# Graph attention with three layer norms: later due times, a third row tile, and one shared turn for the softmax denominators of both head halves

## Chip, cores and metric

The kernel runs on one core of one Trainium2 chip. The metric is the device time of one execution in microseconds (us). Three timed runs of the kernel before gave 3237.86, 3241.72 and 3245.61 us; the median, 3241.72 us, is the time to beat. A fourth, separate execution was recorded by the hardware profiler, and all durations below come from that one.

## What is computed

The input `x` has 8 images of 2048 rows with 256 channels, and `adj` is a 2048 x 2048 adjacency matrix shared by all images. There are 8 heads of 32 channels. Everything is float32.

```python
qkv = einsum('fnc,ck->fnk', x, w_qkv)            # q, k, v, each (f, n, 8, 32)
scores = einsum('fnhd,fmhd->fhnm', q, k) / sqrt(32)
scores = where(adj > 0, scores, -1e9)
attn = softmax(scores, axis=-1)                  # over the 2048 neighbours m
t = einsum('fhnm,fmhd->fnhd', attn, v).reshape(F, N, C)
x1 = layernorm(x + t) * ln1_g + ln1_b
h = relu(x1 @ w1 + b1)
x2 = layernorm(x1 + h @ w2 + b2) * ln2_g + ln2_b
out = layernorm(x + x2)
```

The scores are computed for all pairs, masked, and never written to memory outside the core.

## The kernel before

**Tiling.** The main loop (L599) runs over 1024 *blocks*. A block is one choice of image `f` (8), chunk of 512 query rows `qc` (4), half of the heads `g` (2, four heads each) and 128 neighbours `mb` (16). So 16 blocks make a *half*, 32 blocks make a *chunk* and 128 blocks make an *image*. In each block TensorE makes the scores of four heads (L230, neighbours on the partitions, queries along the free axis), VectorE adds the mask while it takes them out of PSUM (L233, two instructions), ScalarE takes the exponential in place (L237), and TensorE multiplies by the values (L249), adding up in one PSUM bank over the 16 blocks of a half. Scores are issued two blocks ahead (`LEAD`), the exponential one block ahead.

**Denominators.** The softmax denominator is a sum of the exponentials over all 2048 neighbours. Of the 16 score tiles of a half, seven are added into the first one by GpSimd (`POOLED`, L271), two chains of four are added by accumulating DMAs that GpSimd issues (`MOVED`, L268), and one stands alone. The function `denominator` (L297) multiplies the four tiles that remain with a matrix of ones on TensorE (L315, four steps of four matmuls), copies the sum out with ScalarE (`dT`, L317), turns it with four transposes (L321) and takes reciprocals on VectorE (L326), with two small bookkeeping instructions (L327, L328). It does so once for each half, so twice per chunk. A score tile comes from a pool of 12 (`pp`), and the tiles that `denominator` reads are free only after it has read them.

**The row tail.** After the second half of a chunk, `outcome` (L333) turns the attention output (two transposes groups, L352), multiplies it by the reciprocals on VectorE (L353) into a row tile `y` of 512 rows, and GpSimd adds `x` to it with an accumulating DMA (L339). Then `tail` (L357) makes the first norm, the feed-forward (`feed_forward`, L449: two transposes groups, then two groups each for `w1` and `w2`), the second norm, two GpSimd multiplies and adds (L363, L365), another accumulating DMA (L367), the third norm and the store (L370). A norm (L274) takes four statistics on VectorE (L278, L279), a short chain on GpSimd (L283 to L287), and four activations on ScalarE (L290). There are two row tiles (`yp`), so at most two tails are open at once (`ROOM`, L530).

**The order of the work beside the main loop.** All of this, and the projections and transposes that prepare the next image, is written as generators that are kept in the list `fill`, sorted by a due time (L488). In each block `advance` (L504) resumes them. A number that a generator yields is the number of blocks until it goes on. `BANK` means that it needs the one PSUM bank that is left for such work, and a group of matmuls keeps the bank until it is through (`MORE`). `advance` gives each block a credit of 2200, and a step of four 512-column matmuls costs 2048, a group of transposes 1400; so a block takes one step, unless some generator that waits for the bank is past its due time: then the whole group is issued in that block. All engines execute their own instructions in the order in which this loop wrote them.

**Masks.** The mask tiles of the next chunk are loaded by SyncE (`load_mask`, L150), one in every second block of the second half (L600), into a pool of nine tiles (`mkp`); a chunk uses eight.

The lines that the change and the prediction speak of: `denominator` L297 to L331, `outcome` L333, `norm` L274 with its wait L288, `feed_forward` with its wait L472, `tail` with its wait L368, `ROOM` L530, `load_mask` L600, and the constants `SUM` L262 and L341 to L344.

Of the kernel before, what the change touches and what calls it, by code (L numbers as in the profile page):

```python
# [19 lines left out]
P = 128  # L20
H = 8
# [40 lines left out]
def fast_path(ctx, tc, cst, x, adj, out, RS):  # L62
# [5 lines left out]
    dp = ctx.enter_context(tc.tile_pool(name="dp", bufs=1, space=bass.MemoryType.DRAM))  # L68
    mkp = ctx.enter_context(tc.tile_pool(name="mkp", bufs=MB // 2 + 1))
    ld = ctx.enter_context(tc.tile_pool(name="ld", bufs=LD))  # L70
# [13 lines left out]

    ident, identb, wqkv, w1s, w2s = cst["ident"], cst["identb"], cst["wqkv"], cst["w1s"], cst["w2s"]
    state = {"pair": 0, "side": None, "turn": 0, "turned": False, "holder": None, "tails": 0, "credit": 0}
# [47 lines left out]
    def mask_blocks(qc, mc, cv, to=None):  # L134
        for half in range(2):
            yield BANK
            ps = bank(BF16)
            for r in range(2):
                for j in range(TPC):
                    rr = 2 * half + r  # L140
                    nc.tensor.transpose(ps[:, r, j * P:(j + 1) * P], cv[:, j, rr * P:(rr + 1) * P], identb)
            k = 2 * mc + half
            m = to[half] if to else mask_piece(0, qc, k)
            if half:
                nc.vector.tensor_tensor(m, ps, cst["ones"][:, 0:1, None].to_broadcast([P, 2, CH]), ALU.min, saturate=False)
            else:
                nc.scalar.copy(m.bitcast(I8), ps)
            nc.sync.dma_start(MD[qc, k], words(m))
# [70 lines left out]

    PT, O, OT, RC = {}, {}, {}, {}  # L220

# [39 lines left out]
    ENDED = MB - 5  # L261
    SUM = 4  # L262

# [10 lines left out]
    def norm(t, per=1):  # L274
# [12 lines left out]
        nc.gpsimd.tensor_scalar(nb, nb, -1.0, 1.0, op0=ALU.mult, op1=ALU.mult)  # L287
        yield 2  # L288
        for j in range(TPC):
# [7 lines left out]
    def denominator(f, qc, g, ready):  # L297
        grp = (f, qc, g)
        blocks = [ALONE] + [chain[0] for chain in MOVED + (POOLED,)]
        late = {len(blocks) - 1: ready}  # L300
        if (f, qc, g) == items[-1][:3]:
            blocks = [POOLED[0], 11, 12, MOVED[1][0], 13, 14, MOVED[0][0], 15]
            late = {n: len(items) - k for n, k in ((2, 2), (3, 1), (4, 1), (5, 0), (6, 0), (7, 0))}
        yield BANK
        ps = bank()
        for n, block in enumerate(blocks):
            if n:
                yield MORE
            while state["now"] < late.get(n, 0):
                yield WAIT  # L310
            term = PT.pop((f, qc, g, block))
            state["credit"] -= 4 * CH
            for h in range(4):
                r = D * h
                nc.tensor.matmul(ps[r:r + D, :], cst["ones"], term[:, h, :], start=(n == 0), stop=(n == len(blocks) - 1))  # L315
# [6 lines left out]
        if g == 0:  # L322
            RC[f, qc] = op.tile([P, TPC, H], F32, name="rc")
        rc = RC[f, qc]
# [4 lines left out]
        if g == 1:  # L329
            begin = items.index((f, qc, g, LAST)) + SUM + 2  # L330
            start(begin, outcome(f, qc) if (f, qc) != (F - 1, NCK - 1) else finish(f, qc), begin)  # L331

    def outcome(f, qc):  # L333
        yield ROOM
        state["tails"] += 1
        xin = x[f, qc * CH:(qc + 1) * CH, :].rearrange("(p j) c -> p j c", p=P)
        y = yp.tile([P, TPC, C], F32, name="y")
        yield from divide(f, qc, y)
        nc.gpsimd.dma_start(y, xin, accum_op=ALU.add)  # L339
        begin = items.index((f, qc, 1, LAST)) + SUM + 2  # L340
        if (f, qc) == (F - 1, NCK - 2):  # L341
            start(begin + 5, tail(f, qc, y, xin, 2), begin + 8)
        else:
            start(begin + 10, tail(f, qc, y, xin), begin + 26)  # L344

    def divide(f, qc, y):
        rc = RC.pop((f, qc))
        for gg in range(2):
# [5 lines left out]
                                    ps.rearrange("p (j h d) -> p j h d", h=4, d=D),  # L354
                                    rc[:, :, 4 * gg:4 * gg + 4, None].to_broadcast([P, TPC, 4, D]), ALU.mult)

    def tail(f, qc, y, xin, per=1):  # L357
# [9 lines left out]
        nc.gpsimd.dma_start(z, xin, accum_op=ALU.add)  # L367
        yield 7  # L368
        yield from norm(z, per)
# [67 lines left out]
    def finish(f, qc):  # L437
        y = yp.tile([P, TPC, C], F32, name="y")
        xr, xb = state["rows"]
# [4 lines left out]
        while both:  # L444
            for e in list(both):
                if next(e, both) is both:
                    both.remove(e)

    def feed_forward(y):  # L449
# [21 lines left out]
        state["turned"] = False  # L471
        yield 1  # L472
        z = y
# [30 lines left out]
    def advance(t, finish=False):  # L504
# [15 lines left out]
        for e in list(fill):  # L520
            while e[2] is not None and e[0] <= t and e is not state["holder"]:
# [14 lines left out]
    items = [(f, qc, g, mb) for f in range(F) for qc in range(NCK) for g in range(2) for mb in range(MB)]  # L536
    LEAD = 2
    FRAME = 2 * NCK * MB
# [221 lines left out]
def kernel(  # L760
# [47 lines left out]
    make_identity(nc, cst["ident"])  # L808
    cst["identb"] = const.tile([P, P], BF16, name="identb")
    nc.vector.tensor_copy(cst["identb"], cst["ident"])  # L810
    cst["ones"] = const.tile([P, D], F32, name="ones")
    nc.gpsimd.memset(cst["ones"], 1.0)
    cst["mhalf"] = const.tile([P, TPC], F32, name="mhalf")
    nc.gpsimd.memset(cst["mhalf"], -0.5)
    RS = const.tile([P, 2, TPC, H // 2], F32, name="RS")
    nc.gpsimd.memset(RS[:, 0], 0.0)
# [5 lines left out]
    with tc.tile_pool(name="gd", bufs=1) as gd, \  # L822
# [6 lines left out]
        ps = gdp.tile([2, 1], F32, name="okp")  # L829
        nc.tensor.matmul(ps, ok, cst["ones"][:, 0:1], start=True, stop=True)  # L830
# [3 lines left out]
        nc.tensor.matmul(ps1, n_ok, cst["ones"][0:2, 0:1], start=True, stop=True)  # L834
        bad = gd.tile([1, 1], I32, name="bad")
# [35 lines left out]
```

## Time and profile before

| | us |
|---|---:|
| median of three runs | 3241.72 |
| the profiled execution's own time | 3246.02 |
| its span (first to last instruction) | 3244.1 |
| start to the first block's value product | 98.9 |
| 1023 spacings from that one to the last block's value product | 3097.6 |
| from there to the end | 47.6 |
| mean and median spacing of two blocks | 3.03 and 2.92 |

The spacing of blocks is read off the starts of the value products (L249) in the timeline; an image is 128 of them. Image 0 took 373.8 us, images 1 to 6 took 388.4 us on average, and image 7 took 393.5 us. The granted TensorE clock was 0.985 of full speed over the span and 1.00 in most chunks.

### The profile page before, as it was taken

The page shows a single profiled execution, that of the slowest core. Times are in us where ns is not written, and L with a number is a line of the kernel's source. Part 1 is how long each engine was busy: PE and PEld are TensorE (multiplying, and loading weights), DVE is VectorE, ACT ScalarE, POOL GpSimd, SP SyncE. Part 2 cuts the span into 40 slices and gives each one's busy share as a digit, 9 for nine tenths or more (in the row PEclk, how much of TensorE's full clock was granted, in tenths as well). Part 3 has the DMA queues.
Part 4 walks back from the last instruction along what each step waited for, and adds up shares of the span by engine and source line. Part 5 has one row for each costly group of instructions (what it writes and reads, how often), then busy time and mean ns, then how long its engine had stood idle before and what let it go on. Part 6 is the DMA issues. An engine that isn't in the chain of part 4 may idle for free.

```text
span 3244.1 us, 68406 instructions
## 1 busy us (share of the span) xinstructions
PE 3109.4 (96%) x28996; PEld 979.0 (30%) x28996; DVE 2735.7 (84%) x3203; ACT 2435.8 (75%) x1941; POOL 2592.2 (80%) x1358
## 2 busy tenths in 40 slices
PE   7899999999999999999999999999999999998985
PEld 4222333223332233322233323323233323332222
DVE  4888888888888888888988888888888888888975
ACT  3667778777777777778777778777778777777774
POOL 0568888888878888788887888888888788878884
PEclk8899999999999999999999999999999999999998
DMA  9688779778879788788787879878788878877763
GB/s 320 145 181 185 183 176 199 178 177 196 181 176 207 171 188 193 159 195 200 178 181 174 185 174 221 177 167 198 173 192 197 177 168 198 181 171 161 166 145 86
DMA packets 153240, 590.52 MB, mean 182 GB/s; under 512 B 15040, under 2 KB 67776, under 8 KB 103904
## 3 DMA queue, kind: packets, MB, share of 16 engines
q0 software_dynamic: 64416, 434.80, 66.9%
q1 hardware_dynamic: 87696, 149.98, 13.1%
q8 instruction: 229, 3.75, 0.4%
q10 hardware_dynamic: 816, 1.31, 0.1%
q14 instruction: 83, 0.68, 0.1%
HBM read 146.67 MB, written 37.75 MB: 57 GB/s over the span
## 4 chain that ended last, share of the span: by engine, by line
PE 75%; DVE 7%; POOL 5%; issue 4%; DMA 4%; ACT 2%; DVEq 0%; POOLq 0%; ACTq 0%
PE s L230 27%; PE x L249 24%; PE x L54 14%; PE x L315 6%; DVE p L233 6%; PE x L95 4%; DMA p<-p 3%; POOL p L271 2%; ACT p L237 1%; DMA mask<-md 1%; POOL y L365 1%; DVE st L278 1%; POOL y L363 0%; POOL y L461 0%; POOL y L459 0%
## 5 line engine op out<-in xcount | busy, mean ns | idle before, releaser
L233 DVE TENSOR_TENSOR p<-s,mask 128x1024 f32<-128x1024 f32 x2048 | 2409.3, 1218 | 372.7 <-PE s L230 209.9
L237 ACT ACTIVATE p<-p 128x2048 f32<-128x2048 f32 x1024 | 1956.1, 1910 | 521.4 <-DVE p L233 465.6
L271 POOL TENSOR_TENSOR p<-p 128x2048 f32<-128x2048 f32 x381 | 1825.5, 4793 | 223.7 <-ACT p L237 221.3
L230 PE MATMUL s<-qT,kT 32*128 32x512 f32 x8192 | 1173.8, 643 | 40.8 <-DVE p L233 35.9
L249 PE MATMUL x<-p,v 128*32 128x512 f32 x8192 | 1096.0, 607 | 16.7 <-ACT p L237 16.4
L268 POOL DMA_DIRECT2D p<-p x383 | 359.3, 956 | 306.9 <-ACT p L237 88.3
L230 PEld LDWEIGHTS s<-qT,kT 32*128 32x128 f32 x8192 | 321.1, 183 | 644.7 <-DVE p L233 587.2
L249 PEld LDWEIGHTS x<-p,v 128*32 128x32 f32 x8192 | 161.6, 108 | 797.8 <-issue 310.6
L315 PE MATMUL x<-p,ones 128*32 128x512 f32 x2080 | 268.2, 594 | 17.9 <-POOL p L271 11.1
L290 ACT ACTIVATE y<-y,nb,rs 128x256 f32<-128x256 f32 x372 | 218.7, 590 | 40.4 <-POOL nb L287 40.4
L54 PE MATMUL x<-in,wqkv 128*32 128x512 f32 x1888 | 243.5, 592 | 0.0
L278 DVE BATCH_NORM_STATS2 st<-y 128x6 f32<-128x256 f32 x372 | 154.9, 416 | 5.1 <-DMA y<-in_x_dram 5.1
L54 PE MATMUL x<-turned,w1s 128*32 128x512 f32 x992 | 123.5, 596 | 0.4 <-ACT in L166 0.4
L54 PE MATMUL x<-w2s,hT 128*32 128x256 f32 x2016 | 121.8, 382 | 2.1 <-DVE y L483 2.1
L54 PEld LDWEIGHTS x<-wqkv,in 128*32 128x32 f32 x3584 | 102.2, 110 | 63.4 <-issue 58.9
L315 PEld LDWEIGHTS x<-p,ones 128*32 128x32 f32 x2080 | 66.3, 110 | 178.2 <-issue 140.4
L54 PE MATMUL x<-wqkv,in 128*32 128x128 f32 x3584 | 117.3, 273 | 0.0
L54 PEld LDWEIGHTS x<-in,wqkv 128*32 128x32 f32 x1888 | 61.7, 110 | 140.9 <-issue 113.7
L284 POOL TENSOR_TENSOR rs<-rs,mhalf 128x4 f32<-128x4 f32 x93 | 96.3, 1036 | 7.8
L54 PEld LDWEIGHTS x<-w2s,hT 128*32 128x32 f32 x2016 | 65.4, 111 | 75.0 <-issue 33.0
L363 POOL TENSOR_TENSOR y<-y,g2r 128x1024 f32<-128x1024 f32 x31 | 82.5, 2663 | 5.3 <-ACT y L290 5.3
L461 POOL TENSOR_TENSOR y<-y,be1b2r 128x1024 f32<-128x1024 f32 x31 | 83.0, 2679 | 0.6
(116 smaller groups left out, 1335.7 us busy)
## 6 DMA issues: line engine op xcount, KB each, us to landing
p<-p POOLq DMA_DIRECT2D x383, 1024.0 KB, 10.4
in<-xd SPq DMA_DIRECT2D x87, 512.0 KB, 10.6
mask<-md SPq DMA_DIRECT2D x248, 128.0 KB, 7.9
y<-in_x_dram POOLq DMA_DIRECT2D x62, 512.0 KB, 8.1
p<-in_adj_dram SPq DMA_DIRECT2D x16, 1024.0 KB, 10.7
out_dram<-y SPq DMA_DIRECT2D x31, 512.0 KB, 6.2
in<-in_x_dram SPq DMA_DIRECT2D x29, 512.0 KB, 15.5
xd<-in SPq DMA_DIRECT2D x28, 512.0 KB, 11.2
```

Source lines behind the costliest of these rows:

```text
L54: nc.tensor.matmul(out[r:r + D], lhsT[:, r:r + D], rhs, start=start, stop=stop)
L95: nc.tensor.transpose(ps[:, j * P:(j + 1) * P], s, ident)
L230: nc.tensor.matmul(ps2[half][:, j, :], KT[f, mb // TPC, g][r:r + D, (mb % TPC) * P:(mb % TPC + 1) * P], QT[f, qc, g][r:r + D, :], start=Tr ...
L233: nc.vector.tensor_tensor(pt[:, 2 * half:2 * half + 2, :], ps, MK[f, qc, mb // 2][:, mb % 2, None, :].to_broadcast([P, 2, CH]), ALU.add)
L237: nc.scalar.activation(PT[item], PT[item], AF.Exp, scale=1.0 / math.sqrt(D))
L249: nc.tensor.matmul(O[grp][r:r + D, :], V[f, mb // TPC, g][:, mb % TPC, r:r + D], PT[item][:, h, :], start=(mb == 0), stop=(mb == LAST))
L268: nc.gpsimd.dma_start(PT[f, qc, g, chain[0]], PT.pop(item), accum_op=ALU.add)
L271: nc.gpsimd.tensor_tensor(first, first, PT.pop(item), ALU.add)
L278: nc.vector.bn_stats(st, t[:, j, :])
L284: nc.gpsimd.tensor_tensor(rs, rs, cst["mhalf"], ALU.pow)
L290: nc.scalar.activation(t[:, j, :], t[:, j, :], AF.Identity, bias=nb[:, j:j + 1], scale=rs[:, j:j + 1])
L315: nc.tensor.matmul(ps[r:r + D, :], cst["ones"], term[:, h, :], start=(n == 0), stop=(n == len(blocks) - 1))
```

## The change

Five things are changed together.

1. *Denominators.* The matrix of ones becomes `halves`, with two versions: for the first half the first 16 of 32 columns are ones and the rest zeros, for the second half the last 16. The first half's sums are copied by ScalarE into the row tile of the chunk, which is now allocated at this point. For the second half VectorE adds those sums to the new ones as it takes them out of PSUM, into a part of the score tile that was read first; this is turned once, and one reciprocal serves all eight heads.
2. *Row tiles.* Three instead of two, and three open tails allowed. `ROOM` is asked for in the first half's denominator instead of in `outcome`.
3. *Waits.* `SUM` goes from 4 to 5; a norm waits `max(5 - per, 2)` blocks instead of 2 before its activations; the feed-forward waits 3 instead of 1 before `w2`; the tail waits `11 - 2 * per` instead of 7 before the third norm; tails start 12 blocks after `begin` instead of 10 and are due after 30 instead of 26. All tails of the last image take statistics two to a block (`per` = 2) and start after 8, due after 12. The last chunk's own routine `finish` yields a block after each round.
4. *Masks.* One mask tile fewer (eight), and each load is issued six blocks later.
5. *Small space.* The bfloat16 identity lies in the tile `oT1` instead of one of its own.

```diff
-    mkp = ctx.enter_context(tc.tile_pool(name="mkp", bufs=MB // 2 + 1))
+    mkp = ctx.enter_context(tc.tile_pool(name="mkp", bufs=MB // 2))
-    yp = ctx.enter_context(tc.tile_pool(name="yp", bufs=2))
+    yp = ctx.enter_context(tc.tile_pool(name="yp", bufs=3))
...
-    SUM = 4
+    SUM = 5
...
-        yield 2
+        yield max(5 - per, 2)
         for j in range(TPC):
             nc.scalar.activation(t[:, j, :], t[:, j, :], AF.Identity, bias=nb[:, j:j + 1], scale=rs[:, j:j + 1])
...
+        spare = None
+        if g == 0:
+            yield ROOM
+            state["tails"] += 1
+            Y[f, qc] = yp.tile([P, TPC, C], F32, name="y")
+        half = Y[f, qc][:, 0:2, :].rearrange("p a c -> p (a c)")
...
             term = PT.pop((f, qc, g, block))
+            spare = spare or term
...
-                nc.tensor.matmul(ps[r:r + D, :], cst["ones"], term[:, h, :], start=(n == 0), stop=(n == len(blocks) - 1))
-        dT = op.tile([P, CH], F32, name="dT")
-        nc.scalar.copy(dT, ps)
+                nc.tensor.matmul(ps[r:r + D, :], cst["halves"][:, g, :], term[:, h, :], start=(n == 0), stop=(n == len(blocks) - 1))
+        if g == 0:
+            nc.scalar.copy(half, ps)
+            return
+        dT = spare[:, 0, :]
+        nc.vector.tensor_tensor(dT, ps, half, ALU.add)
         yield 1
         yield BANK
         ps = bank()
         transposes(ps, [dT[:, j::TPC] for j in range(TPC)])
-        den = ps.rearrange("p (j c) -> p j c", c=P)[:, :, ::D]
-        nc.vector.reciprocal(rc[:, :, 4 * g:4 * g + 4], den)
+        den = ps.rearrange("p (j c) -> p j c", c=P)[:, :, ::D // 2]
+        nc.vector.reciprocal(rc, den)
...
-        if (f, qc) == (F - 1, NCK - 2):
-            start(begin + 5, tail(f, qc, y, xin, 2), begin + 8)
+        if f == F - 1:
+            start(begin + 8, tail(f, qc, y, xin, 2), begin + 12)
         else:
-            start(begin + 10, tail(f, qc, y, xin), begin + 26)
+            start(begin + 12, tail(f, qc, y, xin), begin + 30)
...
-        yield 7
+        yield 11 - 2 * per
         yield from norm(z, per)
...
         state["turned"] = False
-        yield 1
+        yield 3
...
-                elif e[2] == TURNED and state["turned"] or e[2] == ROOM and state["tails"] == 2:
+                elif e[2] == TURNED and state["turned"] or e[2] == ROOM and state["tails"] == 3:
...
-        if g == 1 and mb % 2 and (f + 1 < F or qc + 1 < NCK):
-            load_mask(f + (qc + 1) // NCK, (qc + 1) % NCK, mb // 2)
+        uf, uqc, ug, umb = items[max(t - LATE, 0)]
+        if ug == 1 and umb % 2 and (uf + 1 < F or uqc + 1 < NCK):
+            load_mask(uf + (uqc + 1) // NCK, (uqc + 1) % NCK, umb // 2)
```

More of the change, by code (lines that the diff above doesn't have):

```diff
@@ L83, in fast_path @@
     ctx.enter_context(tc.manual_schedule())
-    ident, identb, wqkv, w1s, w2s = cst["ident"], cst["identb"], cst["wqkv"], cst["w1s"], cst["w2s"]
+    ident, wqkv, w1s, w2s = (cst[n] for n in ("ident", "wqkv", "w1s", "w2s"))
+    identb = op.tile([P, CH], F32, name="oT1")[:, 0:P // 2].bitcast(BF16)
+    nc.vector.tensor_copy(identb, ident)
     state = {"pair": 0, "side": None, "turn": 0, "turned": False, "holder": None, "tails": 0, "credit": 0}
@@ L144, in mask_blocks @@
             if half:
-                nc.vector.tensor_tensor(m, ps, cst["ones"][:, 0:1, None].to_broadcast([P, 2, CH]), ALU.min, saturate=False)
+                nc.vector.tensor_tensor(m, ps, cst["halves"][:, 0:1, 0:1].to_broadcast([P, 2, CH]), ALU.min, saturate=False)
             else:
@@ L217, in project @@
         give(xT)
-    PT, O, OT, RC = {}, {}, {}, {}
+    PT, O, OT, RC, Y = {}, {}, {}, {}, {}
     def scores(item):
@@ L321, in denominator @@
         transposes(ps, [dT[:, j::TPC] for j in range(TPC)])
-        if g == 0:
-            RC[f, qc] = op.tile([P, TPC, H], F32, name="rc")
-        rc = RC[f, qc]
-        den = ps.rearrange("p (j c) -> p j c", c=P)[:, :, ::D]
-        nc.vector.reciprocal(rc[:, :, 4 * g:4 * g + 4], den)
+        rc = RC[f, qc] = op.tile([P, TPC, H], F32, name="rc")
+        den = ps.rearrange("p (j c) -> p j c", c=P)[:, :, ::D // 2]
+        nc.vector.reciprocal(rc, den)
         nc.vector.tensor_tensor(RS[:, 0], RS[:, 0], den, ALU.add)
         nc.vector.tensor_tensor(RS[:, 1], RS[:, 1], den, ALU.min)
-        if g == 1:
-            begin = items.index((f, qc, g, LAST)) + SUM + 2
-            start(begin, outcome(f, qc) if (f, qc) != (F - 1, NCK - 1) else finish(f, qc), begin)
+        begin = items.index((f, qc, g, LAST)) + SUM + 2
+        start(begin, outcome(f, qc) if (f, qc) != (F - 1, NCK - 1) else finish(f, qc), begin)
     def outcome(f, qc):
-        yield ROOM
-        state["tails"] += 1
         xin = x[f, qc * CH:(qc + 1) * CH, :].rearrange("(p j) c -> p j c", p=P)
-        y = yp.tile([P, TPC, C], F32, name="y")
+        y = Y.pop((f, qc))
         yield from divide(f, qc, y)
@@ L354, in divide @@
                                     ps.rearrange("p (j h d) -> p j h d", h=4, d=D),
-                                    rc[:, :, 4 * gg:4 * gg + 4, None].to_broadcast([P, TPC, 4, D]), ALU.mult)
+                                    rc[:, :, gg::2, None].to_broadcast([P, TPC, 4, D]), ALU.mult)
     def tail(f, qc, y, xin, per=1):
@@ L437, in finish @@
     def finish(f, qc):
-        y = yp.tile([P, TPC, C], F32, name="y")
+        y = Y.pop((f, qc))
         xr, xb = state["rows"]
@@ L447, in finish @@
                     both.remove(e)
+            yield 1
     def feed_forward(y):
@@ L536, in fast_path @@
     items = [(f, qc, g, mb) for f in range(F) for qc in range(NCK) for g in range(2) for mb in range(MB)]
-    LEAD = 2
+    LEAD, LATE = 2, 6
     FRAME = 2 * NCK * MB
@@ L808 @@
     make_identity(nc, cst["ident"])
[L809 to L812, printed above, removed]
     cst["mhalf"] = const.tile([P, TPC], F32, name="mhalf")
     nc.gpsimd.memset(cst["mhalf"], -0.5)
-    RS = const.tile([P, 2, TPC, H // 2], F32, name="RS")
+    cst["halves"] = const.tile([P, 2, D], F32, name="halves")
+    nc.gpsimd.memset(cst["halves"], 0.0)
+    for g in range(2):
+        nc.gpsimd.memset(cst["halves"][:, g, g * D // 2:(g + 1) * D // 2], 1.0)
+    RS = const.tile([P, 2, TPC, H], F32, name="RS")
     nc.gpsimd.memset(RS[:, 0], 0.0)
@@ L829 @@
         ps = gdp.tile([2, 1], F32, name="okp")
-        nc.tensor.matmul(ps, ok, cst["ones"][:, 0:1], start=True, stop=True)
+        nc.tensor.matmul(ps, ok, cst["halves"][:, 0, 0:1], start=True, stop=True)
         n_ok = gd.tile([2, 1], F32, name="nok")
@@ L833 @@
         ps1 = gdp.tile([1, 1], F32, name="okq")
-        nc.tensor.matmul(ps1, n_ok, cst["ones"][0:2, 0:1], start=True, stop=True)
+        nc.tensor.matmul(ps1, n_ok, cst["halves"][0:2, 0, 0:1], start=True, stop=True)
         bad = gd.tile([1, 1], I32, name="bad")
```

## The prediction

> **What bounds the kernel now.** I read the page's busy times first, then the chain of waits, then the waits by engine, then the timeline of a plain stretch and of the places where the blocks are late.
>
> ```profile
> PE 3109.4 (96%) x28996; PEld 979.0 (30%) x28996; DVE 2735.7 (84%) x3203; ACT 2435.8 (75%) x1941; POOL 2592.2 (80%) x1358
> ...
> PE 75%; DVE 7%; POOL 5%; issue 4%; DMA 4%; ACT 2%; DVEq 0%; POOLq 0%; ACTq 0%
> ```
>
> TensorE is nearly always busy and carries three quarters of the chain, but VectorE is at 84%: little is free. The timeline of a plain stretch, TensorE first, then VectorE:
>
> ```profile
> 2235.77 1.06 PE L249 MATMUL x<-p,v 128*32 128x512 f32 x8
> 2236.65 1.04 PE L315 MATMUL x<-p,ones 128*32 128x512 f32 x8
> 2237.62 1.14 PE L230 MATMUL s<-qT,kT 32*128 32x512 f32 x8
> 2238.69 1.06 PE L249 MATMUL x<-p,v 128*32 128x512 f32 x8
> 2239.69 0.75 PE L95 MATMUL x<-ident,dT 128*128 128x128 f32 x4
> ...
> 2241.44 1.06 PE L249 MATMUL x<-p,v 128*32 128x512 f32 x8
> ```
> ```profile
> 2235.97 2.35 DVE L233 TENSOR_TENSOR p<-s,mask 128x1024 f32<-128x1024 f32 x2
> 2238.25 0.42 DVE L278 BATCH_NORM_STATS2 st<-y 128x6 f32<-128x256 f32 x1
> 2238.70 0.18 DVE L279 BATCH_NORM_AGGREGATE mv<-st 128x2 f32<-128x6 f32 x1
> 2238.83 2.36 DVE L233 TENSOR_TENSOR p<-s,mask 128x1024 f32<-128x1024 f32 x2
> ...
> 2243.92 0.68 DVE L353 TENSOR_TENSOR y<-x,rc 128x512 f32<-128x512 f32 x1
> 2244.52 2.34 DVE L233 TENSOR_TENSOR p<-s,mask 128x1024 f32<-128x1024 f32 x2
> ```
>
> From the starts: a block with one side step takes 2.92 (2235.77 to 2238.69), one with a turn 2.75 (to 2241.44). The step itself is 0.97 (2236.65 to 2237.62), so a bare block is 1.95 of TensorE and a turn 0.80. Elsewhere in the timeline a block with two steps takes 3.79, one with a turn of other tiles 2.65, one with nothing 2.5. VectorE, start to start: mask adds 2.28 (2235.97 to 2238.25), one statistic 0.58 (to 2238.83), one division 0.60 (2243.92 to 2244.52). So a block with a statistic needs 2.86 of VectorE: it just fits beside a step, not beside a turn. Four late places:
>
> ```profile
> 1499.68 1.06 PE L315 MATMUL x<-p,ones 128*32 128x512 f32 x8 [1.38 <-POOL p L271]
> 1538.83 0.69 DVE L483 TENSOR_TENSOR y<-x,y 128x512 f32<-128x512 f32 x1 [2.13 <-POOL y L461]
> 2994.44 0.60 ACT L290 ACTIVATE y<-y,nb,rs 128x256 f32<-128x256 f32 x1 [6.90 <-POOL nb L287]
> 3128.36 0.43 DVE L278 BATCH_NORM_STATS2 st<-y 128x6 f32<-128x256 f32 x1 [5.13 <-DMA y<-in_x_dram]
> ```
>
> Each time an engine stands at a side instruction that was issued too soon, and the main loop behind it waits. Taking every spacing against the usual one of its kind, images 1 to 6 lose 35.0 in this way, 5.8 each; image 7 loses 14.7 in three places.
>
> [...] So a norm's activation issued too soon holds the exponential behind it; the trace agrees (6.90 above, with the scores' VectorE idle after it). [...] the trace has 690 for L483. That prices the new addition into `dT`. [...] mask adds wait 2.0 for L271 and 1.7 for the accumulating DMAs in all.
>
> **The change, part by part**, for images 1 to 6.
>
> *Denominators.* One turn and one set of L326 to L328 go per chunk. TensorE saves 0.80 x 4 = 3.2 per image. ScalarE loses one 0.59 copy per chunk, covered (75% busy). VectorE gains 0.69 and loses 0.24 + 0.11 + 0.16 per chunk, about even. The new addition waits for the last of four steps, with the next two mask adds queued behind it. I place it by the due times below: in three chunks of four it falls in a forced block of two steps (3.79 against 2.28 + 0.69), so nothing; without that cover up to 0.4.
>
> *Waits.* I wrote out by hand which step falls in which of the 128 blocks, from the generators' yields and due times; the same done with the old numbers puts denominators, turns and feed-forward of the chunk at 1732 where the trace has them. Old stalls: activations now come four blocks (11.7) after the GpSimd chain is issued instead of two, `w2` six blocks after L461, and L363 and L365 move from blocks 12 to 17 of a chunk, before the first half's denominator, to 22 and 23, after it. I take 4.3 of the 5.8 as gone (bounds 3 to 5.8). What is late next:
>
> - The feed-forward now starts at block 30 of a chunk instead of 25 and has a gap of three blocks. The second half's denominator, started one block after the chunk's end, falls in this gap (blocks 5 to 7), and `w2` follows (8, 9). So the denominator's turn and the two turns of `outcome` stand at blocks 10, 11 and 12, exactly where the second norm takes its statistics (10 to 13). VectorE then needs 3.26, 3.46, 3.46 and 2.86 (adds, statistic, and 0.40 for the reciprocals or 0.60 for a division) = 13.04; TensorE 2.75 x 3 + 2.92 = 11.17. VectorE may lag by about 0.4, since score PSUM is three pairs deep: 1.45 lost. Before, these turns came after the statistics. Three chunks of an image are so; the fourth, where older projections push in, loses about 0.8: together 5.1. Not seen before; from below 0, if the lag is made up by the two-step blocks ahead of it, from above 2.0 per chunk.
> - Blocks without any step: two per image in the trace, five by hand (one at 60, four from 89, when the next input must wait for a buffer that an earlier projection keeps). Each leaves 2.5 - 1.95 = 0.55 of TensorE unused: +1.65.
> - Score tiles: the kept tile and the later denominators hold one to two of 12 longer. Counted from first write to last use, at most 11 are in use before. From below 0, from above one wait of 2 per chunk; I take 0.25, so 1.0 per image.
>
> Per image -3.2 - 4.3 + 5.1 + 1.65 + 1.0 = +0.25, for six images +1.5.
>
> *Row tiles.* By hand a tail closes 109 to 110 blocks after its chunk's start, and the fourth asks at 113: `ROOM` never holds. Cost nothing; if it did, score tiles would be held.
>
> *Masks.* A load's slot is free two blocks later and SyncE reaches it up to eight later: from 42 to 52 ahead of use (issue to first mask add) to some 20 to 35; landing takes 8.1 in the median, 24.8 at most. Nothing, at worst a few single waits. SyncE's stores of outputs and inputs move ahead of the loads.
>
> *Small space.* The identity and the matrix of ones are made before the first block; under 0.5.
>
> *Image 7.* Its three stalls go (-14.7), as do four turns that mostly leave empty blocks (4 x 0.25 = -1). But with two statistics per block and starts 32 blocks apart, the third norm of one tail and the first of the next fall in the same two blocks, 78 and 79, and 110 and 111: VectorE 2.28 + 4 x 0.58 = 4.60 against 2.5, less the lag: +3.8 each time, 7.5. Their activations, four beside one exponential (1.91 + 4 x 0.59 = 4.27 against 2.92), fall together too: +2 each time, 4. The first tail starts two blocks (5.8) after its accumulating DMA, which lands in 8.1 after issue and must first pass GpSimd's 4.8 additions: +5 (2 to 7). Pairs of statistics in other blocks +2.5, the crossing as above +1.5. Sum +4.8.
>
> *Start and end.* Image 0 has its first tail late: +0.5. At the end the last-but-one tail has its second and third norm after the last block, about 33 of latency beside the 47.6 of `finish`: 0, between -4 and +5.
>
> Sum +7 (1.5 + 4.8 + 0.5): 3246.0 becomes 3253. The profiled execution lies 4.3 above the median of the runs; I state the median: 3249.
>
> **Rivals.** *Faster:* the turns and the statistics don't collide, because VectorE makes up its lag or the denominators come elsewhere. Then 5.1 + 1.0 per image don't arise, nor half of image 7's 15: 7 - 37 - 8 = -38, so 3204. For it: VectorE is at 84 of 97 in a chunk, and all old stalls are met. Against: 2.86 beside 2.75 leaves nothing at a turn. It decides once the turns lie more than a block after block 13. *Score tiles run out:* one wait of 2 or more for GpSimd or a DMA in each of 31 chunks, +55: 3297. For it: 11 of 12 used; against: the old waits are 3.7 in all. *Masks late:* landing 24.8 with a lead of 20 at some of 31 chunk starts, +15: 3264; SyncE reports waits up to 60.5.
>
> **Numbers.** A difference under 0.2%, 6.5, can't be told from none; the three runs spread over 7.8. Forecast 0.57 (its own range 3230 to 3268), faster rival 0.24, score tiles 0.13, masks 0.06. Faster is the rival and a little of the forecast's lower side: 0.29; within 0.2% 0.19; slower 0.52. The range runs from the faster rival's centre to short of the score tiles': 3205 to 3287.
>
> **What would show it.** Right: no more waits of L290 for L287 or of L315 for L271; in a chunk, L278 and L353 in the same blocks 10 to 12 with spacings of 3.0 or more and L230 waiting for L233; image 7 with blocks of over 4 near its 78th and 110th. Wrong: turns at spacings of 2.75 with statistics beside them, or images well under 388 (faster), mask adds waiting for L271, a DMA or a mask (slower).

## The result, and the profile after

| | before | after |
|---|---:|---:|
| median time, us | 3242.98 | 3332.41 |
| range of the timed runs | 3237.86 to 3245.61 | 3327.19 to 3334.4 |
| the profiled execution's span | 3244.1 | 3325.4 |
| image 0 / images 1 to 6 on average / image 7 | 373.8 / 388.4 / 393.5 | 375.4 / 400.0 / 404.7 |
| first value product / from the last one to the end | 98.9 / 47.6 | 97.8 / 47.6 |

The change makes the kernel slower: the ratio of the times is 1.0275, with a 95% interval of 1.0257 to 1.0293. The forecast was 3249, its range 3205 to 3287. It missed by 83 us. That it also said slower is no success: its +7 was the small remainder of savings and costs several times larger. The profiled execution of after is the fastest of its four; of the 81.3 that the two spans differ, images 1 to 6 give 69.9 (6 x 11.65), image 7 gives 11.2 and image 0 gives 1.6, and the start takes back 1.1.

The page of after, first its busy times, then the chain of waits by engine and by line:

```profile
PE 3113.7 (94%) x28868; PEld 962.2 (29%) x28868; DVE 2751.6 (83%) x3139; ACT 2423.0 (73%) x1909; POOL 2589.5 (78%) x1360
...
PE 33%; DMA 22%; POOL 19%; DVE 11%; issue 8%; ACT 3%; DVEq 0%; POOLq 0%; ACTq 0%
DMA p<-p 22%; POOL p L273 13%; PE s L232 13%; PE x L251 10%; DVE p L235 9%; PE x L54 7%; PE x L324 3%; ACT p L239 2%; POOL y L372 1%; POOL y L467 1%; POOL y L370 1%; POOL rs L286 1%; PE x L97 1%; POOL p L270 1%; DVE y L360 1%
```

The busy times hardly move, and 128 matmuls fewer are issued. The chain changes its nature: TensorE falls from 75% to 33%, and the makers of the sums, the accumulating DMAs (`p<-p`) and GpSimd, rise from 4% and 5% to 22% and 19%. The list of waits says where they are felt (us in total, times, the longest):

```profile
DVE p L235 <- DMA p<-p: 127.5, 61, 6.0
...
DVE p L235 <- POOL p L273: 12.2, 17, 1.1
...
ACT y L292 <- POOL nb L289: 6.1, 5, 1.9
```

The mask add L235 is the first instruction that writes a score tile, so here it waits until the last user of that tile is through; these waits were 1.7 and 2.0 before. (Each half has six additions, L273, and six accumulating DMAs, L270. The tile that is added comes free with the addition or the landing.) The third line is an old stall that the longer waits were to end: it was 40.4 and is 6.1.

The place is the beginning of chunk 15 (image 3), whose block 0 starts at 1572.8. The timeline of GpSimd there (start, duration, instruction, and in brackets the idle time before it and what ended that):

```profile
1563.26 0.85 POOL L270 DMA_DIRECT2D p<-p  x1 [1.29 <-issue]
1563.84 4.88 POOL L273 TENSOR_TENSOR p<-p 128x2048 f32<-128x2048 f32 x1
1571.80 0.87 POOL L270 DMA_DIRECT2D p<-p  x1 [3.08 <-issue]
1572.38 9.55 POOL L273 TENSOR_TENSOR p<-p 128x2048 f32<-128x2048 f32 x2
1581.89 2.38 POOL L467 TENSOR_TENSOR y<-y,g1r 128x1024 f32<-128x1024 f32 x1
1584.35 2.38 POOL L469 TENSOR_TENSOR y<-y,be1b2r 128x1024 f32<-128x1024 f32 x1
1586.68 4.57 POOL L273 TENSOR_TENSOR p<-p 128x2048 f32<-128x2048 f32 x1
1591.18 0.88 POOL L270 DMA_DIRECT2D p<-p  x1
...
1594.29 0.93 POOL L270 DMA_DIRECT2D p<-p  x1 [0.28 <-issue]
```

The two additions at 1572.38 belong to blocks 13 and 15 of the half before: GpSimd enters the chunk some 7 us behind. It works without a gap to 1591.18, and its next addition, block 3's, starts at 1586.68, five us after block 3 began and just before block 5 does. In between lie the feed-forward's L467 and L469, 4.8 us that no score tile waits for. The two accumulating DMAs of blocks 4 and 5 are issued at 1591.18 and 1594.29, with a norm's short chain (L285 to L289, 1.9 us) between them; they land at 1598.74 and 1604.55. VectorE at the same time:

```profile
1591.28 2.36 DVE L235 TENSOR_TENSOR p<-s,mask 128x1024 f32<-128x1024 f32 x2 [1.05 <-POOL p L273]
1593.56 0.68 DVE L329 TENSOR_TENSOR p<-x,y 128x512 f32<-128x512 f32 x1
1598.86 2.36 DVE L235 TENSOR_TENSOR p<-s,mask 128x1024 f32<-128x1024 f32 x2 [4.62 <-DMA p<-p]
1601.13 0.68 DVE L491 TENSOR_TENSOR y<-x,y 128x512 f32<-128x512 f32 x1
1604.74 2.36 DVE L235 TENSOR_TENSOR p<-s,mask 128x1024 f32<-128x1024 f32 x2 [2.92 <-DMA p<-p]
```

Twice it stands for a tile whose sum has not landed: block 9's mask add (scores are made two blocks ahead) starts 0.1 after the landing of block 4's tile, block 10's 0.2 after that of block 5's. Blocks 7 and 8 take 7.4 and 5.3 instead of 3.79.

The pool is not empty meanwhile. Counted from first write to last use, nine of the 12 tiles are in use when the first of these two waits begins, eight at the second, and at most 11 at each of the 68 such waits over 0.3 us in images 1 to 7. Which tile a block takes over stands in the program: block 9 waits 4.62 for its own while three others are unused. In this chunk, blocks 8, 9 and 10 take over the tiles of blocks 3, 4 and 5, only five blocks old; in the kernel before, where the second half's denominators come earlier, the same blocks take tiles 10, 24 and 7 blocks old. A tile that is only five blocks old is ready in time when GpSimd is, and late when GpSimd is late: chunk 1 of an image has the same five, its additions come in time, and its blocks 7 and 8 lose nothing.

A few blocks on, the collision that the forecast named:

```profile
1610.80 2.35 DVE L235 TENSOR_TENSOR p<-s,mask 128x1024 f32<-128x1024 f32 x2
1613.07 0.42 DVE L280 BATCH_NORM_STATS2 st<-y 128x6 f32<-128x256 f32 x1
1613.52 0.18 DVE L281 BATCH_NORM_AGGREGATE mv<-st 128x2 f32<-128x6 f32 x1
1613.62 0.66 DVE L360 TENSOR_TENSOR y<-x,rc 128x512 f32<-128x512 f32 x1
1614.19 2.35 DVE L235 TENSOR_TENSOR p<-s,mask 128x1024 f32<-128x1024 f32 x2
```

From mask add to mask add VectorE needs 3.39 with a statistic and a division between them; 3.46 was forecast.

### The profile page after: what moved, and what is told of

It is laid out like the page before. It is cut to its first block, busy times and chain, and to the rows that moved or that the text cites. A ratio compares the mean times of both kernels' runs of the same rounds, so it can differ in the third digit from the quotient of the medians.

```text
span 3325.4 us, 67974 instructions
## 1 busy us (share of the span) xinstructions
PE 3113.7 (94%) x28868; PEld 962.2 (29%) x28868; DVE 2751.6 (83%) x3139; ACT 2423.0 (73%) x1909; POOL 2589.5 (78%) x1360
## 3 DMA queue, kind: packets, MB, share of 16 engines
q1 hardware_dynamic: 87696, 149.98, 13.1%
## 4 chain that ended last, share of the span: by engine, by line
PE 33%; DMA 22%; POOL 19%; DVE 11%; issue 8%; ACT 3%; DVEq 0%; POOLq 0%; ACTq 0%
DMA p<-p 22%; POOL p L273 13%; PE s L232 13%; PE x L251 10%; DVE p L235 9%; PE x L54 7%; PE x L324 3%; ACT p L239 2%; POOL y L372 1%; POOL y L467 1%; POOL y L370 1%; POOL rs L286 1%; PE x L97 1%; POOL p L270 1%; DVE y L360 1%
## 5 line engine op out<-in xcount | busy, mean ns | idle before, releaser
L235 DVE TENSOR_TENSOR p<-s,mask 128x1024 f32<-128x1024 f32 x2048 | 2411.6, 1219 | 465.5 <-PE s L232 199.7
L273 POOL TENSOR_TENSOR p<-p 128x2048 f32<-128x2048 f32 x381 | 1825.7, 4792 | 281.4 <-ACT p L239 278.2
L270 POOL DMA_DIRECT2D p<-p x383 | 388.6, 1023 | 327.0 <-issue 91.0
L324 PE MATMUL x<-p,halves 128*32 128x512 f32 x2080 | 265.7, 594 | 16.1 <-DMA p<-p 16.1
L292 ACT ACTIVATE y<-y,nb,rs 128x256 f32<-128x256 f32 x372 | 217.0, 590 | 6.1 <-POOL nb L289 6.1
L324 PEld LDWEIGHTS x<-p,halves 128*32 128x32 f32 x2080 | 66.9, 110 | 175.6 <-issue 143.3
L370 POOL TENSOR_TENSOR y<-y,g2r 128x1024 f32<-128x1024 f32 x31 | 78.7, 2540 | 5.6 <-ACT y L292 5.6
L281 DVE BATCH_NORM_AGGREGATE mv<-st 128x2 f32<-128x6 f32 x372 | 67.8, 182 | 12.7
```

Of the source, the lines that this page charges most:

```text
L235: nc.vector.tensor_tensor(pt[:, 2 * half:2 * half + 2, :], ps, MK[f, qc, mb // 2][:, mb % 2, None, :].to_broadcast([P, 2, CH]), ALU.add)
L270: nc.gpsimd.dma_start(PT[f, qc, g, chain[0]], PT.pop(item), accum_op=ALU.add)
L273: nc.gpsimd.tensor_tensor(first, first, PT.pop(item), ALU.add)
L292: nc.scalar.activation(t[:, j, :], t[:, j, :], AF.Identity, bias=nb[:, j:j + 1], scale=rs[:, j:j + 1])
L324: nc.tensor.matmul(ps[r:r + D, :], cst["halves"][:, g, :], term[:, h, :], start=(n == 0), stop=(n == len(blocks) - 1))
L370: nc.gpsimd.tensor_tensor(z, z, rows(cst["g2r"]), ALU.mult)
```

## Experiments

Seven theories stand in the expectations. K: the tile kept for the turn makes the pool run out. D: the second half's denominators are read too late. V: statistics and turns collide on VectorE. G: GpSimd makes the sums that free score tiles, and the new waits put its other work where it is already behind. N: the longer wait of the norm shifts the second norm's work on GpSimd into the next half. P: how the steps fall into blocks, together with VectorE, carries what G does not. D2 is D whatever GpSimd does. The kernel before took 3243 to 3244 in every comparison, so medians can be set side by side.

### The tile, the place of the denominators, or the waits

**in_row.** The sum goes back into the row tile.

```diff
-        dT = spare[:, 0, :]
+        dT = half
         nc.vector.tensor_tensor(dT, ps, half, ALU.add)
```

> The changed kernel, except that the second half's sum is written over the first half's sum in the row tile, so that no score tile is kept for the turn. Theory K (the kept score tile makes the pool run out): the late blocks 7 and 8 of chunks 2 and 3 go, some 7.4 us per image in the trace of after, so 50 in all: 3275 to 3290, and mask adds wait for an accumulating DMA or a GpSimd addition for under 60 (127.5 and 61 in after). Theory D (the tiles are held because the second half's denominators are read late, in blocks 4 to 6): only blocks 7 and 8 could gain, and the waits move to the blocks after: 3315 to 3332. Theory V (statistics and turns collide on VectorE, as I forecast): no gain, 3325 to 3335.

Measured: 3317.1 (1.0222, 1.0205 to 1.0239), 15 less than after and in D's range. K is wrong as the main cause. Its list of waits:

```profile
DVE p L235 <- DMA p<-p: 104.6, 53, 6.0
```

The tile is worth a sixth of the loss; the pool runs out without it.

**early_den.** Every denominator is due five blocks earlier, the second half's so ahead of `w1`.

```diff
-            start(t + 2, denominator(f, qc, g, t + SUM), t + SUM + 4)
+            start(t + 2, denominator(f, qc, g, t + SUM), t + 4)
```

> The changed kernel, except that the second half's denominator is due at t + 4 instead of t + SUM + 4, so that it goes ahead of the feed-forward's w1. Theory K: the tile is still kept for a turn, but in blocks 4 to 6, when four tiles are already free: half of the loss or more returns, under 3300, but not more than in_row gives. Theory D: nearly all of the waits for score tiles go, in blocks 1 to 3 too: 3265 to 3285. Theory V: the turns now stand ahead of the statistics or beside others of them; the waits for DMA and GpSimd stay as they are, and the time is within 15 of after's 3332.

Measured: 3314.12 (1.0212, 1.0195 to 1.023), in no theory's range. The waits have moved; the same list:

```profile
PEld x L324 <- DMA p<-p: 85.3, 40, 4.1
...
PE x L324 <- DMA p<-p: 52.4, 34, 3.2
...
DVE p L235 <- DMA p<-p: 18.1, 11, 3.2
```

L324 is the denominators' matmul. D is right about the tiles: with the denominators read earlier, blocks 8, 9 and 10 of chunk 15 take over tiles 23, 23 and 7 blocks old, the mask adds' waits nearly go, and so do the collisions of blocks 9 to 12. But it is wrong about the time, which falls by 18 only. Read earlier, L324 stands for the sums itself, which are not there yet: blocks 0 to 5 lose 10.9 us per image (blocks 0 to 8 lost 13.1 in after). Another 4.9 per image is new, at blocks 26 and 27 of one chunk, a turn that waits for its input load. So what is to be read is late, not only the reading.

**old_waits.** The third part of the change is undone: `SUM` 4, waits of 2, 1 and 7, tails at 10/26, the last image and `finish` as before.

> The changed kernel with all five waits and the tails' start and due times as before (SUM 4, 2, 1, 7, 10/26, and the last image as before); the new denominators, the third row tile and the mask loads stay. Theory K: the tile is kept here too; if that alone is enough, 3290 to 3330. Theory D: the waits make the denominator late (blocks 4 to 6 instead of 2 to 5), so they are the cause: 3225 to 3250, about the kernel before, less the saved turns. Theory V: the same as D in time, but with VectorE's spacings of 3.2 and 3.4 gone and the waits for score tiles still there in part.

Measured: 3233.18 (0.997, 0.9959 to 0.9981). All the loss, and a little more, lies in the waits: 99 us between this kernel and after. The time is D's, but early_den, which undoes D's part alone, has shown that D's reason isn't enough. GpSimd at the same place, where chunk 15 starts at 1533.8:

```profile
1520.88 2.72 POOL L466 TENSOR_TENSOR y<-y,g1r 128x1024 f32<-128x1024 f32 x1
1523.22 4.91 POOL L273 TENSOR_TENSOR p<-p 128x2048 f32<-128x2048 f32 x1
1527.75 2.71 POOL L468 TENSOR_TENSOR y<-y,be1b2r 128x1024 f32<-128x1024 f32 x1
...
1530.67 9.89 POOL L273 TENSOR_TENSOR p<-p 128x2048 f32<-128x2048 f32 x2
1542.22 4.56 POOL L273 TENSOR_TENSOR p<-p 128x2048 f32<-128x2048 f32 x1 [1.67 <-ACT p L239]
```

The feed-forward's pair (L466 and L468 here) is over before the chunk starts. GpSimd is about 6 us behind at the chunk's end here too, but by 1540.6 it is through with the old half and waits for the exponential of block 3.

**old_den.** The changed kernel with the old denominators, each half copied into its own quarter of the row tile and turned by itself.

```diff
...
-        if g == 0:
-            nc.scalar.copy(half, ps)
-            return
-        dT = spare[:, 0, :]
-        nc.vector.tensor_tensor(dT, ps, half, ALU.add)
+        dT = half
+        nc.scalar.copy(dT, ps)
...
```

> The changed kernel with the denominators of before: each half is summed with a matrix of ones, copied by ScalarE and turned by itself. The copy goes into a quarter of the row tile, which is there already, so no score tile is kept. New waits, three row tiles and late mask loads stay. Theory K: no tile is kept, so the waits for score tiles fall under 60 and the time comes to 3275 to 3295 (3.2 us per image for the second turn are paid again). Theory D: the lateness comes from the waits, which stay: 3320 to 3350. Theory V: the collisions stay as well: 3330 to 3355.

Measured: 3333.49 (1.0278, 1.0261 to 1.0295), like after, and mask adds wait 116.1 for the DMAs. So neither the shared turn nor the tile kept for it causes the loss, as old_waits says from the other side. Nor does the shared turn gain anything here.

### GpSimd

**no_additions.** The feed-forward's multiplication by `g1` and its addition of `be1 + b2` on GpSimd are left out; every other instruction stays in its block, and the blocks take over the same tiles as in after.

```diff
-        nc.gpsimd.tensor_tensor(y, y, rows(cst["g1r"]), ALU.mult)
         yield 1
-        nc.gpsimd.tensor_tensor(y, y, rows(cst["be1b2r"]), ALU.add)
```

> The changed kernel without GpSimd's multiplication and addition in the feed-forward (L467, L469), so the residual keeps neither g1 nor be1 + b2; all yields stay, and so every other instruction stays in its block. Theory G (GpSimd makes the sums that free score tiles; the new waits put these 4.8 us into blocks 0 to 3, where it is 7 to 9 us behind, so the sums of the half before land late): GpSimd is under 2 us behind at blocks 3 to 7, mask adds wait for a DMA or GpSimd under 40 in all, and the time is 3235 to 3265. Theory D2 (the denominators' place, blocks 4 to 6, is late whatever GpSimd does): the waits at blocks 7 and 8 stay, 3305 to 3330.

Measured: 3275.06 (1.0101, 1.0083 to 1.0119), 57 less than after and 10 above the range for G. The waits for DMAs came to 59.6, not under 40. In images 1 to 6 the lateness of blocks 6 to 8 falls from 7.4 us per image to 0.1, and that of blocks 0 to 4 stays (5.7 and 6.1). (Lateness is the spacing above the usual one of a block with the same steps.) In chunks 2 and 3 of these images GpSimd starts block 3's addition 0.9 us before and 0.4 after that block's value product, on average, where it was 4.0 and 5.2 after it in after. D2, which wanted blocks 7 and 8 to stay late, is wrong.

**after_no_four.** L370 and L372, the second norm's multiplication by `g2` and addition of `be2`, are left out as well.

> no_additions with GpSimd's second pair left out too (L370, L372: the second norm's g2 and be2), so that GpSimd has 9.6 us less per chunk; yields stay. Theory G (GpSimd is behind at the chunk's boundary and its sums free the score tiles): what is left in no_additions at blocks 1 to 3 (about 5 per image) goes as well; 3235 to 3262, mask adds wait for a DMA or GpSimd under 15, and blocks 10 to 12 keep their 3.2 and 3.4 (VectorE). Rival P (the step packing and VectorE's collisions carry the rest): no further gain, 3268 to 3278.

Measured: 3268.83 (1.0084, 1.0067 to 1.01). In time this is what P said; in place it is what G said. Blocks 0 to 4 now lose 0.3 per image and blocks 6 to 8 nothing, so nearly all of the 13.1 that blocks 0 to 8 lost in after is gone, though the mask adds' waits for DMAs stay at 27.1, not under 15. A new wait has come up instead, a turn of input rows that waits for their load:

```profile
PEld x L97 <- DMA in<-in_x_dram: 30.8, 6, 5.8
...
DVE p L235 <- DMA p<-p: 27.1, 18, 3.5
```

It costs about 6 per image at blocks 28 and 29 of one chunk. Why that load is late was not tried.

**old_waits_no_four.** The control: the same four instructions out of old_waits.

> The same four GpSimd instructions left out of old_waits (3233). Theory G: only the stalls at blocks 30 and 31 of chunk 1 and those of L292 behind L289 can go, 5 per image: 3195 to 3215. So the two sets of waits, 99 apart with the four instructions, are 30 to 55 apart without them. Rival P: the gap stays above 65.

Measured: 3206.85 (0.9897, 0.9881 to 0.9914). The two sets of waits are 62 apart without the four instructions, 99 with them: between what G and P allowed. Of the 62, the new load wait is about 30 by that list, and the collisions of blocks 9 to 12 are about 24 (4.2 per image against 0.3), a part that P named.

**moved_additions.** Nothing is left out; the pair is only issued later.

```diff
-        nc.gpsimd.tensor_tensor(y, y, rows(cst["g1r"]), ALU.mult)
         yield 1
-        nc.gpsimd.tensor_tensor(y, y, rows(cst["be1b2r"]), ALU.add)
...
         state["turned"] = False
-        yield 3
+        yield 2
+        nc.gpsimd.tensor_tensor(y, y, rows(cst["g1r"]), ALU.mult)
+        yield 1
+        nc.gpsimd.tensor_tensor(y, y, rows(cst["be1b2r"]), ALU.add)
```

> The changed kernel with the feed-forward's two GpSimd instructions (L467, L469) issued in the last two of the three blocks ahead of w2, instead of between the turns and w1, so some five blocks later; nothing is left out, and TensorE's order stays. Theory G (GpSimd's order decides when the sums land): the sums of blocks 3 to 5 go ahead of the 4.8 us, the stalls at blocks 7 and 8 shrink by half or more and those at blocks 1 to 3 a little, 3280 to 3310. Rival P (packing and VectorE): 3325 to 3340. If w2's L491 then waits for L469 instead: 3325 or more, with that wait in the list.

Measured: 3345.83 (1.031, 1.0295 to 1.0325). It is slower, by the third case. Its list of waits:

```profile
DVE y L492 <- POOL y L481: 90.5, 30, 8.3
...
DVE p L235 <- DMA p<-p: 48.3, 38, 3.3
```

The waits for tiles fall from 127.5 to 48.3, and block 7 of chunk 15 takes 3.8 instead of 7.4; but now `w2`'s addition on VectorE waits for GpSimd's L481. Images 1 to 6 take 399.0 on average, 1.0 less than in after, and image 7 takes 435.0. So the place of 4.8 us on GpSimd decides which instruction waits for GpSimd.

### Which wait

Each of these is old_waits (3233.18) with one wait put back, or after (3332.41) with one undone. **only_tail_start** puts back 12/30 (8/12 in the last image); **only_norm_wait** puts back `yield max(5 - per, 2)`.

> old_waits (3233) with one of the new waits put back: the tails start 12 blocks after begin and are due after 30 (8 and 12 in the last image). Theory G: this alone puts the feed-forward four blocks later, its GpSimd additions into blocks 31 to 3, and brings most of the loss: 3285 to 3320. Theory N (the norm's wait of four blocks shifts the second norm's GpSimd work into the next half): 3230 to 3255.

> old_waits (3233) with one of the new waits put back: the norm waits four blocks instead of two before its activations. The stall of the activation behind GpSimd's chain (L292 on L289, 40.4 in all) goes, 25 us or so. Theory G: the feed-forward is held by its due time and moves little, so 3205 to 3235. Theory N: 3280 to 3310.

Measured: 3249.1 (1.0019, 1.0011 to 1.0027) and 3312.9 (1.0209, 1.0185 to 1.0233): the first lies in N's range, the second 3 above it, and G's ranges miss both. But the trace of only_norm_wait shows another wait than the one N stands for:

```profile
POOL p L270 <- DMA p<-p: 138.6, 45, 6.7
...
DVE y L490 <- POOL y L468: 111.2, 28, 9.0
```

The feed-forward, two blocks later with its own wait before `w2` still at one, has its addition on GpSimd issued right ahead of `w2`. Mask adds wait 4.1 for DMAs there, so it is not after's loss on a smaller scale; it is GpSimd being late for another customer.

**all_but_tail_start** and **all_but_norm_wait** undo one wait in the changed kernel.

> The changed kernel with the tails' start and due times alone as before (10 and 26, the last image as before). Theory G: the additions come back to blocks 28 to 31 or so, the waits for score tiles fall by more than half, 3225 to 3265. Theory N: 3300 to 3325.

> The changed kernel with the norm's wait alone as before (two blocks). The tail keeps its start and due times of 12 and 30, so the feed-forward stays where it is, with its additions in blocks 31 to 3. Theory G: the second norm's GpSimd pair comes two to four blocks earlier, ahead of the crowded end of the chunk, so GpSimd is less behind there: 3265 to 3300. If the norm's wait is the whole cause: 3230 to 3255. If the feed-forward's place is the whole cause: 3315 or more.

Measured: 3418.92 (1.0539, 1.0517 to 1.0561) and 3379.33 (1.0429, 1.0408 to 1.0451), 87 and 47 more than after. I had expected both to be faster than after; only the last case of all_but_norm_wait, with its "or more", holds the number. Both lists show GpSimd and the DMAs again. The one of all_but_tail_start:

```profile
POOL p L270 <- DMA p<-p: 253.8, 99, 5.7
...
DVE p L235 <- DMA p<-p: 148.0, 75, 4.3
```

The waits do not add: undone alone, each makes things worse.

**third_norm_wait**, **first_norm_wait** and **second_norm_wait** give four blocks to one of the three norms only.

```diff
-    def norm(t, per=1):
+    def norm(t, per=1, wait=2):
...
-        yield max(5 - per, 2)
+        yield wait
...
+        yield from norm(z, per, 4)
         nc.sync.dma_start(out[f, qc * CH:(qc + 1) * CH, :].rearrange("(p j) c -> p j c", p=P), z)
```

> old_waits with four blocks instead of two ahead of the activations of the third norm alone, behind which no GpSimd work of the tail follows. Theory G: the stalls of L292 behind L289 (40.4 in all, blocks 27, 30 and 31) go and no GpSimd instruction moves: 3200 to 3222. Theory N (any longer norm wait costs, as only_norm_wait's 80 would suggest): 3250 or more.

> old_waits (3233) with four blocks instead of two ahead of the activations of the first norm alone. The feed-forward follows two blocks later, and its GpSimd addition (L468) is issued right ahead of w2, which adds to the same rows. Theory G: L490 waits for L468 as in only_norm_wait (111.2 there, 37.4 in old_waits for other reasons), 3280 to 3330. If the second norm is the cause: 3225 to 3245.

> old_waits with four blocks instead of two ahead of the activations of the second norm alone; its GpSimd pair (L370, L372) and the accumulating DMA (L374) come two blocks later, and the third norm with them. Theory G: GpSimd is one to three us later in blocks 16 to 25, 3225 to 3260, less than the first norm's. If the second norm is the cause of only_norm_wait's 80: 3280 or more.

Measured: 3200.36 (0.9878, 0.986 to 0.9896), 3260.26 (1.0055, 1.0034 to 1.0075) and 3270.37 (1.0095, 1.0073 to 1.0118). The third norm's longer wait saves 33; the wait of L292 for L289 falls from 40.4 to 3.2. Those of the other two, behind which GpSimd instructions of the tail follow, cost 27 and 37. In first_norm_wait L490 waits 50.8 for L468, as expected, though the time is 20 below what I gave it. In second_norm_wait L292 waits 92.3 for L289, more than the 40.4 of old_waits. Its time is 10 above G's range. The three single effects sum to about 31, all three together give 80.

**all_but_last_image** gives the last image its old tails in the changed kernel.

> The changed kernel with the last image's tails as before (statistics one to a block, start 12 and due 30; the last-but-one chunk 5 and 8). My forecast gave the new arrangement 19.5 of collisions (7.5, 4, 5, 2.5 and 0.5) against 14.7 saved; image 7 took 404.7 with it and 386.5 with the waits of before. Collisions as forecast: image 7 loses 10 to 20, 3312 to 3324. If GpSimd's lag makes image 7's loss too: 3325 to 3340.

Measured: 3343.07 (1.0317, 1.0296 to 1.0338), 11 slower than after and above both ranges; image 7 takes 411.2 instead of 404.7, and the end 52.0 instead of 47.6. The new arrangement of the last image, which I had given a net loss of 4.8, gains under these waits.

### The version to keep

**third_norm_and_start** adds to third_norm_wait the sum in the row tile, and the last-but-one chunk's tail at 8/11.

> third_norm_wait, with the second half's sum kept in the row tile as in in_row, and with the last-but-one chunk's tail started 8 blocks after begin (due 11), so that its statistics do not stand waiting for the accumulating DMA (6.5 at block 10 of the last chunk in old_waits). If the parts add: 3 to 10 below third_norm_wait, 3193 to 3215; if the kept tile is never short with the old waits, only the 5 or so of the start.

Measured: 3196.7 (0.9865, 0.9847 to 0.9883): faster than both kernels, 46 below before. Image 7 takes 378.5 instead of 383.5 in third_norm_wait, the 5 of the start; the row tile adds nothing that shows. The chain of the page:

```profile
PE 74%; DVE 16%; issue 3%; POOL 2%; DMA 2%; ACT 1%; DVEq 0%; ACTq 0%; POOLq 0%
```

GpSimd is as busy as ever (2588.5) and carries 2% of the chain.

**best_old_den** is that version with the denominators of before.

> third_norm_and_start (3197) with the denominators of before: each half summed with ones, copied by ScalarE into its own quarter of the row tile and turned by itself. My forecast's 3.2 per image, and 1 in image 7: 3197 + 8 x 3.2 = 3223, 3215 to 3230. If the saved turn only leaves emptier blocks behind, as it does in image 7: 3198 to 3212.

Measured: 3221.43 (0.9924, 0.9909 to 0.9939). Where next to nothing waits for GpSimd, one turn for both halves saves 24.7, or 3.1 per image; in after itself old_den shows no such saving.

## Why the forecast was wrong, step by step

Per image, images 1 to 6; lateness is counted as above.

| step | forecast | measured |
|---|---:|---:|
| denominators: one turn fewer per chunk | -3.2 | -3.1 (best_old_den; hidden in after, see old_den) |
| old stalls gone | -4.3 | -5.8 (none is left in after) |
| statistics beside turns, blocks 9 to 12 | +5.1 | +5.0 |
| three more blocks without a step | +1.65 | +1.65 (5.0 for 2.0 before, at 0.55) |
| score tiles | +1.0 | +13.1 in blocks 0 to 8, +0.6 at block 24 |
| sum | +0.25 | +11.45; the spacings grew by 11.65 |

**The step that failed** is the one on score tiles: "From below 0, from above one wait of 2 per chunk; I take 0.25, so 1.0 per image." Blocks 0 to 8 lost 13.1 per image in place of 1.0; even the upper end, 8, was too low. The count beside it holds: at most 11 of 12 tiles are in use before, and at most 11 at the waits of after. Wrong was to let that count decide. A block waits for the one tile that it takes over, and that tile comes free when its sum is made or has landed. The later denominators made some of these tiles only five blocks old, and GpSimd, which makes or issues all sums, was late with these (blocks 6 to 8, 7.4) and with tiles of the half before (blocks 0 to 4, 5.7). The same prediction says that `w2` comes six blocks after L461, that the feed-forward starts at block 30 instead of 25, and that L363 and L365 move to blocks 22 and 23. I priced these moves on TensorE, VectorE and ScalarE and gave GpSimd none of it. But each moved pair is 4.8 to 5.0 us on an engine that in three chunks of four is on average 6 to 10 us behind in the last four blocks (start of its addition less the start of the block that issued it), before the change and after. Before, the feed-forward's pair was mostly over by the chunk's end; after, it delays the sums at the beginning of the next chunk, when two halves hold their tiles. no_additions, after_no_four and moved_additions show this. Of the other theories the tile kept gives 15 of the 89 us (in_row), the denominators' place 18 (early_den) and the turn none (old_den).

Lines of the trace of before that should have led there:

```profile
L233 DVE TENSOR_TENSOR p<-s,mask 128x1024 f32<-128x1024 f32 x2048 | 2409.3, 1218 | 372.7 <-PE s L230 209.9 <-issue 53.4 <-ACT y L290 42.6
...
L271 POOL TENSOR_TENSOR p<-p 128x2048 f32<-128x2048 f32 x381 | 1825.5, 4793 | 223.7 <-ACT p L237 221.3
...
L268 POOL DMA_DIRECT2D p<-p x383 | 359.3, 956 | 306.9 <-ACT p L237 88.3 <-issue 80.9 <-DMA p<-p 75.5
```

One addition of two score tiles took GpSimd 4.79 on average, about twice the 2.44 that VectorE's two mask adds took over as many elements (2 x 1.218). And all 383 accumulating DMAs are in GpSimd's own stream, among these additions: at the place shown above from after, the one at 1591.18 starts just as the addition of 4.57 ahead of it ends (1586.68 to 1591.25).

**The rivals.** *Score tiles run out* was the right kind of wait, given 0.13 and 3297. It was priced as one wait of 2 per chunk, where chunks 2 and 3 of an image lose about 5 each, so its centre and the range's upper end (3287) were both too low. Its +55 was besides counted from 3242, where the masks' +15 was counted from 3249; from the same 3249 it stands at 3304. Of the sign that the forecast named for a slower result, one part came, mask adds that wait for a DMA. Of the faster rival's two conditions neither came: the turns do collide with the statistics. *Masks late*: no mask add of after waits for a mask load; the 60.5 that was quoted for SyncE is the wait of a store, and the mask loads' longest was 55.9.

**Row tiles, start and end.** No wait for a row tile shows up. The end takes 47.6 in both kernels, as forecast; the start gained 1.1.

**Image 7.** Collisions stand where they were put: blocks 14 to 16 and 19 to 20 of its chunks 2 and 3 are late by 1.6 to 2.4 each in most cases. But the forecast's +4.8 was against a plain image. Image 7 also has waits like the other images' (2.4 at block 2, 2.1 at block 40), and all_but_last_image shows that the old arrangement would now be worse.

Left open: the late input load in after_no_four and early_den, and why the single waits' effects don't add, beyond what the lists of waits name.

## What to carry over

An engine that isn't the bound and has a fifth of its time free can still be the one that sets when buffers come free, as GpSimd did in after (busy for 78%, with mask adds waiting 127.5 for the DMAs that it issues and 12.2 for its additions); look at how far its instructions lag behind the blocks that issued them, not at its share. When a wait is lengthened, go through every later instruction of that routine on every queue, GpSimd's and its DMAs' too, and ask whose result is delayed where they land; lengthen first the wait behind which nothing follows, as the third norm's here (33 saved). Counting the buffers in use is not enough (at most 11 of 12 were, at 68 waits): find which older buffer each new one takes over, and when its producer will be through under the new order.

## What the runs showed of the hardware

Two things were not expected. TensorE is busy for 94% in after, yet carries 33% of the chain: its busy time hardly differs (3109.4 before, 3113.7 after), and 77 us of the longer span are added idle time. A small part of the loss may come from the granted clock, which was lower after some of the idle stretches, as in these two lines of after's timeline (1.14 and 1.74 us), the same eight matmuls without and with a wait:

```profile
1593.30 1.14 PE L232 MATMUL s<-qT,kT 32*128 32x512 f32 x8
...
1600.14 1.74 PE L232 MATMUL s<-qT,kT 32*128 32x512 f32 x8 [2.97 <-DVE p L235]
```

The granted clock was 1.00 from 1588 to 1600, 0.64 from 1600 to 1602, 0.51 from 1602 to 1604, and 1.00 again from there. In images 1 to 6 the trace of after has eight stretches at half the clock, 30.7 us in all, and that of before two, 6.8 us; each stands beside an idle stretch of TensorE of 1.8 us or more, though not every such stretch has one. An estimate from this: half of the 24 us that they differ, 12 us or 2.0 per image, is the most that the clock can add to the 11.65. No run here separates it from the waits that it follows.

And the landing time of the accumulating DMAs is no longer in after than before, 10.0 us in the median and 10.4 (10.0 in in_row, 10.5 in early_den, 10.4 in old_waits, 9.9 in old_den and 10.5 in the fastest, third_norm_and_start): in after they were late because they were issued late, not because they took longer.
